# Eight tiles for unsearched attention weights, four for keys and values, in a planned transformer kernel

## The chip, the cores and the metric

The kernel runs on one core of one Trainium2 chip. Its metric is the device time of one execution in microseconds. Three runs of the kernel before gave 1355.88, 1356.01 and 1357.18 us; the median is 1356.01 us.

The core has four computing engines that run side by side, each through its own list of instructions, in order: TensorE (PE in the profile, with PEld for its weight loads), VectorE (DVE), ScalarE (ACT) and GpSimd (POOL). SyncE (SP) issues the DMA transfers. An engine waits on a semaphore when its next instruction needs something that another engine or a transfer has not finished.

## What is computed

Sixteen sequences (batches) of 256 tokens with 256 channels, 16 heads of 16 channels, all in float32. Every batch goes through two blocks. The first:

```python
m = silu(mod) @ w_ada + b_ada            # nine rows of shifts, scales, gates per batch
h = ln(x) * (1 + sc_msa) + sh_msa
x = x + self_attn(h) * g_msa             # rolled by 64, two windows of 128 tokens
h = ln(x) * (1 + sc_mca) + sh_mca
x = x + topk_cross_attn(h, context) * g_mca   # only the 16 largest scores of 256 per query
h = ln(x) * (1 + sc_mlp) + sh_mlp
x = x + swiglu(h) * g_mlp                # 256 -> 2 x 1024 -> 256
```

The second block is one more attention, over all 256 context tokens, without a search:

```python
xq, xkv = ada_ln(x_q, t, Wss_q), ada_ln(x_kv, t, Wss_kv)
x = x_q + softmax(q k^T / 4) v @ Wp      # q from xq, k and v from xkv
```

So a batch has three attentions: the windowed one ("self"), the searched one ("topk") and the last one ("last"). The two without a search exponentiate whole rows of scores; the searched one first finds the 16 largest scores of each row.

## The kernel before

**The planner.** The kernel does not issue its work as it is written down. Each piece of work, called an op, is recorded with its engine, a cost, the buffers it reads and writes, and a due time. `Plan.order` sorts the ops by due time (never before what they depend on), gives every buffer a tile from a fixed pool of its kind, and `Plan.run` issues them in that order. The due times are the table `DUE` at line 33: for each batch, stage and op one number in thousandths of a batch. One list serves all inner batches ("topk", "self", "prep", "last", "mlp"); batches 0, 1, 14 and 15 have lists of their own. Batch 15 is worked on in two halves of 128 tokens from its search on (`SPLIT`).

The order on every engine is therefore fixed when the program is built. A change of due times changes the order of instructions on all engines and the sequence in which tiles are handed out, but not the set of instructions.

Where the planner sees PE idle for more than 1 us ahead of an op, and a PSUM tile is free, it puts filler matmuls in (line 355, 128x512 on the identity), one per 0.87 us of the gap. They compute nothing that is used.

**The pools.** A kind of tile has a fixed number of copies (line 336 and the lines after it). An op that needs a tile waits until the last user of that copy has finished. Kinds that matter here:

- `pTO`: exponentials of the scores of an attention without search, 128 x 512. A round of four groups of heads (`exponentials`, line 631) fills four of them, and the product with the values (`weighted`, line 600) reads them.
- `k2`, `v`: keys and values. Each batch needs a pair for each of its three attentions.
- `pTT`: the same as `pTO` for the searched attention. `W`: the eight PSUM tiles, one bank each.

**The stages of a batch, by line.** Normalising: DVE statistics (444, 446), POOL (451 to 456), PE transpose (468), ACT (482). Products with weights: 494 (queries, keys), 530 (values), 577 (output projections). Self attention: scores for the row maxima (800), maxima on DVE (607), a small transpose (617), sixteen or eight tiny DMAs per batch that write the maxima into the queries (624), scores again (808), ACT exponentials (631), product with values (600), then DVE transpose and reciprocal (557, 559), POOL division (560), DVE transpose back (567). The last attention is the same with 952 for the first scores and 964 for the second. The searched attention: scores (847), four rounds a batch; each round has four groups, and each group runs MAX8 and MATCH_REPLACE on DVE twice (866, 874, 886, 891), ACT exponentials (879), a POOL product (895), PE transposes (544), an ACT copy (547) and the product with values (600). Feed-forward: 908 (up), ACT 918 to 927, POOL 925 and 928, and 935 (down). Line 935 is the last PE work of a batch's feed-forward and appears once per batch, so it is a convenient mark of the batches in the trace. Additions to x are on POOL (403, 418, 435), gate rows are scaled into weights at 423.

**Shapes on PE.** PE works in three shapes: the full array (products, transposes), four strips of 32 rows at once (scores: 800, 808, 847, 952, 964) and blocks of 17 output columns (600). The planner charges a switch between them:

```python
SWITCH = {128: 0.18, 32: 0.2, 33: 0.12}
```

A run of neighbouring PE instructions of one shape is called a group below. Loads of weights, of inputs, of gate rows and the tiny DMAs of line 624 all go through SP's one queue, in the planned order.

**The start.** Batch 0 has to go through its self attention before its search can begin, and most parameters are still arriving. The order there interleaves the products that make shifts, scales and gates (706 to 784) with the self attentions of batches 0 and 1.

Of the kernel before, what the change touches and what calls it, by code (L numbers as in the profile page):

```python
# [16 lines left out]
P = 128  # L17
B, L, C = 16, 256, 256
# [16 lines left out]
        -9570, -11657, -12085, -9792, -11847, -9363, -8686, -11839, -9345, -8419, -8682, -11836, -9366, -9397, -11886,  # L35
        -9644, -5321, -1682, -2688, -2632, -1153, -5643, -5425, -2469, -2565, -2724, -9446, -1295, -5757, -2172,
        -5835, -675, -1139, -1157, -5588, -2468, -1870, -5581, -1529, -1076, -1532, -1487, -5566, -1154, -5679, -1223,
        -5943, -106, 1074, 1255, 1393, -472, 224, 278, -1105, -1056, -1026, -5942, -321, -5710, 1347, 1352, -140,
        1081, -1522, -5590, -109, 361, 323, -32, -168, 342, -31, 913, 1389, 1308, 1596, 1753, -1138, -5554, -281,
        -5895,  # L40
    ),
    "self0": (
        -845, -8015, -9552, -8319, -8151, -7887, -2534, -12052, -7991, -11742, -12050, -12022, -11948, -11840, -11934,
        -3275, -11907, -3055, -9473, -9474, -9480, -9412, -3266, -5525, -5526, -5397, -5794, -5754, -1042, -734,
        -1323, -12229, -12179, -12027, -12419, -811, -9968, -9962, -7750, -10294, -872, -12484, -12372, -12192,
        -12320, -406, -10294, -9974, -8000, -5892, -279, -10035, -8044,
    ),
    "prep0": (
        -1155, -12001, -636, -12191, -12321, 410, -9381, 350, -10296, -8016, -7945, -7776, 17, -8420, 111, 261, -8435,
    ),  # L50
    "topk0": (
        397, 331, 117, 330, -8436, 336, 120, 355, -10058, 85, 137, 50, -9816, 51, 172, 25, -8473, -533, 366, 299, 554,
        -10042, 500, 388, 278, 408, -10013, 433, 352, 296, 656, -9074, -534, 523, 553, 595, -9922, 702, 689, 761,
        1066, 1337, 361, 191, 92, 596, -9842, 172, 593, 572, -10045, 536, 589, 451, 704, 130, 530, 577, -9912, 553,
        598, 477, 1093, -8997, 391, 619, 485, 774, -9093, 632, 758, 476, 825, -9242, 556, 633, 552, 1151, -9063, 1102,
        1333, 1338, 1363, 1359, 630, 657, 933, 787, -9141, 720, 1016, 886, -9062, 615, 311, 886, 687, 1092, 1065,
        1219, -9072, 827, 1092, 939, 1209, -8960, 1214, 1213, 1241, 1256, 1240, 1042, 1041, 956, 1089, -9068, 1260,
        1219, 558, 1258, 1240, 1243, 1336, 1337, 1323, 1360, 904, 1124, 1206, 1192, -9069, 1267, 734, 1266, 1211,
        1268, 732, 1329, 1167, 1208, 1029, 1273, 1241, 1261, 1270, 535, 1256, 1204, 1273, 1225, 1055, 1076, 1158,
        1334, 1060, 501, 1340, 1341, 1212, 1256, 502, 1330, 1342, 1353, 1342, 1338, 1367, 1253, 115, 1367, 1131, 1375,  # L60
    ),
    "self1": (
        -3755, -2639, -1238, -1452, -6312, -9036, -9099, -8976, -3443, -13366, -1419, -2386, -13023, -13295, -2081,
        -13301, -13346, -1223, -11030, -1380, -6922, -11295, -7021, -7022, -1205, -644, -687, -11297, -657, -640,
        -993, -1086, -420, -11042, -10382, -11043, -10445, -362, -337, -283, -523, -241, -592, -10816, -10820, -10821,
        -10843, -479, -383, -375, -641, -229, -299, -10068, -319,
    ),
    "prep1": (
        -1302, -13228, -265, -10135, -10120, -1180, -9435, 98, 263, -443, 200, 236, 209, 239, -265, 259, 335,
    ),  # L70
    "topk": (
        123, -321, 178, -60, 228, -226, -683, 166, 151, 153, -678, 173, 225, 164, -635, 88, -58, 396, 531, 633, 712,
        554, 222, 292, 305, 462, 289, -59, 382, 222, 445, 282, 432, 200, 547, 563, 21, 734, 631, 647, 342, 857, 536,
        530, 555, 569, 322, 566, 13, 510, 382, 573, 613, 588, 311, 524, 590, 603, 402, 591, 655, 585, 783, 202, 546,
        581, 633, 714, 610, 699, 712, 731, 779, 282, 659, 748, 349, 795, 525, 867, 596, 892, 941, 1119, 720, 807, 874,
        845, -622, 795, 460, 725, 394, 467, 593, 759, 489, 699, 505, 426, 488, 881, 1006, 804, 1080, 1060, 795, 963,
        913, 1113, 539, 794, 738, 345, 960, -663, 805, 736, 810, 965, -669, 1132, 726, 1018, 543, 1171, 914, 983, 912,
        1057, -908, 1011, 652, 1010, -909, 915, 834, 810, 1129, 1005, 453, 1074, -635, 1081, 1109, 376, 1158, 872,
        1032, 1006, 625, 1117, 920, 1017, 1051, 203, 1164, 872, 1060, 1051, 728, 1157, 710, 1190, 1181, 1210, 1226,
        1221, 240, 1264, 1232, 1243,  # L80
    ),
    "self": (
# [3 lines left out]
        -1907, -45,  # L86
    ),
    "prep": (
        9, 49, -1517, -1480, 156, -399, 268, 11, -190, -190, -375, 48, -1623, 245, 64, 65,
    ),  # L90
    "last": (
        1069, 1097, 1199, 1047, 1040, 1256, 1228, 1346, 1352, 1351, 1437, 1151, 2089, 1541, 1652, 1320, 2149, 1938,
# [1023 lines left out]
```

## Time and profile before

| | us |
|---|---|
| median of three runs | 1356.01 |
| the profiled execution, its time | 1355.89 |
| the profiled execution, span from first to last instruction | 1354.0 |
| PE busy | 1323.4 |
| DVE busy | 1213.5 |
| ACT busy | 1018.0 |
| POOL busy | 1026.5 |
| mean granted clock of TensorE, as a share of full speed | 0.993 |
| first line 935 (batch 0) starts | 164.11 |
| distance of two such marks, batches 0 to 12 | 79.27 (mean of twelve) |
| last line 935 (second half of batch 15) starts | 1317.82 |

The page gives for each engine its busy time, and the span in 40 slices; further views give busy times by stretch, single instructions in order of time, the waits of an engine with what ended them, and the chain of work that ended last. In the trace each matmul of the program appears as two records, so that 16 recorded L935 are 8 in the program (the half of a batch), and 32 a whole one. The idle time in square brackets behind a row is the engine's wait just before it, with the engine or transfer whose result ended it. Lines are those of the kernel before; the changed kernel's are two smaller.

### The profile page before, as it was taken

Reading aid. Unit: us, or ns where it says so; the run is one execution under the profiler, and the core shown is the slowest. Engines: PE = TensorE matmul, PEld = TensorE weight load, DVE = VectorE, ACT = ScalarE, POOL = GpSimd, SP = SyncE. Lnnn points to the kernel's source line nnn. Section 1 sums busy time; section 2 is a strip of 40 time slices with the busy share of each in tenths; the row PEclk is TensorE's granted clock in tenths of the full one; section 3 lists DMA queues with packets and bytes.
Section 4 is the critical chain, followed back from the end, with each engine's and each line's share of the span. In section 5 each row is a group of like instructions: output and inputs, shape, how many; then the busy total and the mean of one; then the engine's idle time right before and its main releaser. Section 6 shows DMA issues by size and latency. Waiting matters only on the chain.

```text
span 1354.0 us, 38576 instructions
## 1 busy us (share of the span) xinstructions
PE 1323.4 (98%) x13490; PEld 1029.2 (76%) x13490; DVE 1213.5 (90%) x4358; ACT 1018.0 (75%) x2359; POOL 1026.5 (76%) x1553
## 2 busy tenths in 40 slices
PE   8788999999999999999999999999999999999998
PEld 6566787878778787877878787787878778787885
DVE  5698999999999999999999999999999999999834
ACT  4466778787887878788787877878777787977783
POOL 1566887878788787878878787887878788778862
PEclk9898999999999999999999999999999999999999
DMA  5322001011100101110010111011011001000000
GB/s 166 105 67 95 21 17 26 25 26 33 26 25 18 24 27 26 33 25 21 22 24 27 26 33 26 12 29 24 29 26 34 23 20 33 19 2 2 17 2 18
DMA packets 64160, 42.44 MB, mean 31 GB/s; under 512 B 37763, under 2 KB 56751, under 8 KB 63711
## 3 DMA queue, kind: packets, MB, share of 16 engines
q1 hardware_dynamic: 63967, 39.99, 10.6%
q8 instruction: 107, 1.75, 0.5%
q14 instruction: 86, 0.70, 0.2%
HBM read 35.14 MB, written 4.29 MB: 29 GB/s over the span
## 4 chain that ended last, share of the span: by engine, by line
PE 87%; POOL 2%; DVE 2%; issue 1%; ACT 0%; POOLq 0%; DVEq 0%; ACTq 0%
PE W L908 17%; PE W L494 11%; PE W L600 11%; PE W L935 8%; PE W L544 8%; PE W L577 6%; PE W L530 5%; PE W L964 5%; PE W L952 5%; PE W L847 4%; PE W L468 3%; PE W L808 2%; PE W L800 2%; POOL prT L895 1%; PE W L355 0%
## 5 line engine op out<-in xcount | busy, mean ns | idle before, releaser
L895 POOL TENSOR_TENSOR prT<-rest,prT 128x512 f32<-128x512 f32 x256 | 325.4, 1275 | 31.5 <-DVE rest L891 23.1
L607 DVE TENSOR_REDUCE nm<-W 128x2 f32<-128x512 f32 (+1 forms) x384 | 237.6, 679 | 30.7 <-PE W L800 22.5
L879 ACT ACTIVATE prT<-W,ntop 128x256 f32<-128x256 f32 x512 | 214.0, 497 | 56.0 <-POOL ntop L868 49.1
L908 PE MATMUL W<-xT,w_L_xcond_w_m 128*128 128x256 f32 (+1 forms) x1088 | 251.2, 376 | 0.1
L631 ACT ACTIVATE pTO<-W 128x512 f32<-128x512 f32 (+1 forms) x392 | 199.8, 603 | 48.5 <-PE W L964 35.3
L908 PEld LDWEIGHTS W<-xT,w_L_xcond_w_m 128*128 128x128 f32 x1088 | 187.5, 190 | 61.5 <-ACT pTO L631 13.7
L874 DVE MATCH_REPLACE8 rest<-top,W 128x256 f32<-128x256 f32 x512 | 207.1, 412 | 0.0
L891 DVE MATCH_REPLACE8 rest<-top,rest 128x256 f32<-128x256 f32 x512 | 204.9, 408 | 0.0
L866 DVE MAX8 top<-W 128x8 f32<-128x256 f32 x512 | 184.3, 413 | 13.8 <-PE W L847 12.8
L886 DVE MAX8 top<-rest 128x8 f32<-128x256 f32 x512 | 185.3, 407 | 0.0
L547 ACT ACTIVATE pTT<-W 128x512 f32<-128x512 f32 x256 | 143.9, 628 | 8.3 <-PE W L544 8.3
L544 PE MATMUL W<-ident,prT 128*128 128x128 f32 x1024 | 137.3, 276 | 6.0 <-ACT prT L879 2.9
L925 POOL TENSOR_TENSOR mb<-ma,mb 128x256 f32<-128x256 f32 (+1 forms) x136 | 95.1, 699 | 53.7 <-ACT ma L920 37.3
L544 PEld LDWEIGHTS W<-ident,prT 128*128 128x128 f32 x1024 | 116.9, 141 | 24.0 <-POOL prT L895 3.8
L557 DVE STREAM_TRANSPOSE tr<-W 128x256 f32<-128x256 f32 (+1 forms) x162 | 78.2, 483 | 43.1 <-PE W L600 28.5
L560 POOL TENSOR_TENSOR on<-tr,rec 128x128 f32<-128x128 f32 (+1 forms) x162 | 71.7, 444 | 56.2 <-DVE rec L559 54.4
L935 PE MATMUL W<-w_L_xcond_w_m,h 128*128 128x256 f32 x512 | 113.6, 380 | 0.0
L935 PEld LDWEIGHTS W<-w_L_xcond_w_m,h 128*128 128x128 f32 x512 | 97.0, 190 | 13.8 <-POOL mb L925 0.7
L600 PE MATMUL W<-pTO,v 128*17 128x128 f32 (+1 forms) x2112 | 104.9, 323 | 0.1
L868 POOL TENSOR_SCALAR ntop<-top 128x2 f32<-128x2 f32 x256 | 52.7, 217 | 66.1 <-DVE top L866 61.6
L928 POOL TENSOR_TENSOR h<-h,mb 128x256 f32<-128x256 f32 (+1 forms) x136 | 94.8, 697 | 10.6
L418 POOL TENSOR_TENSOR x<-x,gated 128x512 f32<-128x512 f32 (+1 forms) x49 | 60.1, 1227 | 47.6 <-ACT gated L417 47.5
(129 smaller groups left out, 2665.6 us busy)
## 6 DMA issues: line engine op xcount, KB each, us to landing
gate<-gates SPq DMA_DIRECT2D x48, 256.0 KB
q<-nmT SPq DMA_DIRECT2D x480, 1.0 KB
cx<-in_ctx_dram SPq DMA_DIRECT2D x19, 256.0 KB
cx<-in_ctx_dram SPq DMA_DIRECT2D x104, 32.0 KB
rest<-in_L_xcond_w_ada_dram SPq DMA_DIRECT2D x9, 256.0 KB
x<-in_x_dram SPq DMA_DIRECT2D x16, 128.0 KB
x<-in_x_dram SPq DMA_DIRECT2D x32, 64.0 KB
w_L_xcond_w_m<-in_L_xcond_w_m_dram SPq DMA_DIRECT2D x1, 2048.0 KB
```

Source lines behind the costliest of these rows:

```text
L544: nc.tensor.transpose(w.t[:, ts(n, P)], flat[:, ts(n, P)], ident)
L600: nc.tensor.matmul(po.t[ds(NW * j, DH + 1), ds(q0, nq)], v.t[:, kt, 8 * m + 2 * j + a, :], pT.t.rearrange("p n q -> p (n q)")[:, ds(part, ...
L607: op("DVE", 0.61, lambda j=j, s=s: nc.vector.tensor_reduce(nm.t[:, k, ds(j, groups, step=4)], s.t.rearrange("p (g k) -> p g k", g=groups), ...
L631: op("ACT", 0.24 + q * 0.0005, lambda s=s, pT=pT: nc.scalar.activation(pT.t.rearrange("p n q -> p (n q)")[:, :q], s.t[:, :q], AF.Exp), r=[ ...
L866: nc.vector.max(top.t[:, a, 0:8], s.t[:, ts(a, L)])
L874: nc.vector.match_replace(rest.t[:, a, :], top.t[:, a, 0:8], s.t[:, ts(a, L)], TAKEN)
L879: nc.scalar.activation(pr.t[:, a, :], s.t[:, ts(a, L)], AF.Exp, bias=ntop.t[:, a:a + 1])
L886: nc.vector.max(top.t[:, a, 8:16], rest.t[:, a, :])
L891: nc.vector.match_replace(rest.t[:, a, :], top.t[:, a, 8:16], rest.t[:, a, :], TAKEN)
L895: op("POOL", 1.25, lambda: nc.gpsimd.tensor_tensor(pr.t, rest.t, pr.t, ALU.mult), r=[rest, pr], w=[pr])
L908: nc.tensor.matmul(w.t[:, :q], w_m1.t[:, c, ds(n0, P)], xT.t[:, c, :q], start=c == 0, stop=c == NCC - 1)
L935: nc.tensor.matmul(pp.t[:, ts(k, C)], hs[f].t[:, ts(k, P)], w_m2.t[:, f, :], start=f == 0, stop=f == NHC - 1)
```

## The change

Three pool sizes change, and the whole table of due times is replaced. There are eight tiles of `pTO` instead of five, four of `k2` instead of five, and four of `v` instead of five. In bytes per partition that is three times 2048 more and 4096 and 2176 less. The ops and their costs are the same.

```diff
 DUE = {
     "start": (
-        -9570, -11657, -12085, -9792, -11847, -9363, -8686, -11839, -9345, -8419, -8682, -11836, -9366, -9397, -11886,
+        -9079, -9474, -9247, -7795, -10959, -5686, -7231, -10933, -5595, -5764, -7671, -10944, -8055, -6777, -10987,
...
     "self": (
-        -1852, -383, -551, -1044, -1694, -2506, -2472, -1969, -746, -967, -952, -648, -716, -717, -644, -1050, -620,
+        -1974, -677, -761, -758, -1718, -1767, -1387, -1242, -787, -1974, -758, -688, -1415, -1974, -694, -590, -601,
...
     "mlp14": (
-        -14237, 1120, 1339, 1241, 1316, 1321, 1123, 1316, 1703, -413, -414, 1750, -224, 1638, -410, 1347, 1771, 1753,
+        -12321, 1209, 1239, 1104, 1103, 1325, 1411, 1103, 1534, 1182, 1202, 1524, 1204, 1580, 1410, 1613, 1680, 1475,
...
         "xT": (3, [P, NCC, L]), "q": (2, [P, NCC, L]), "q2": (2, [P, NCC, 2, L]),
-        "k2": (5, [P, NCC, 2, L]), "v": (5, [P, NT, NH, DH + 1]), "gate": (3, [P, 2, C]), "nm": (4, [P, NT, 32]), "nmT": (4, [P, NT, 32]),
+        "k2": (4, [P, NCC, 2, L]), "v": (4, [P, NT, NH, DH + 1]), "gate": (3, [P, 2, C]), "nm": (4, [P, NT, 32]), "nmT": (4, [P, NT, 32]),
         "top": (8, [P, 2, TOPK]), "ntop": (8, [P, 2]), "rest": (5, [P, 2, L]), "prT": (5, [P, 2, L]),
-        "pTT": (5, [P, 4, P]), "pTO": (5, [P, 4, P]), "tr": (3, [P, 16, NW]), "rec": (3, [P, 16]), "on": (3, [P, 16, DH]),
+        "pTT": (5, [P, 4, P]), "pTO": (8, [P, 4, P]), "tr": (3, [P, 16, NW]), "rec": (3, [P, 16]), "on": (3, [P, 16, DH]),
```

All lists of `DUE` are replaced in the same way. In the built program the order changes on all five engines. On PE the main differences are these, in the counts of the program:

- In the middle of the run, per batch: the two halves of the self attention's product with values (L600, 16 each) stand together and not apart, and some transposes (L544), value products (L530) and feed-forward blocks (L908) change places with neighbours.
- At the start: before the first search round, one L723 block, one L530 block and the L744 block of Wp move behind it; only one search round (L847) instead of two stands ahead of the second scores of batch 1 (L808); an L494 block of batch 2 moves ahead of the last transposes (L544) of batch 0's search. SP's queue is reordered with it.
- At the end: one L600 and one L964 block of batch 14 move from before the last L935 to behind it.

## The prediction

> **What bounds the kernel now.** I read the page first: engine shares and the forty slices.
>
> ```profile
> PE 1323.4 (98%) x13490; PEld 1029.2 (76%) x13490; DVE 1213.5 (90%) x4358; ACT 1018.0 (75%) x2359; POOL 1026.5 (76%) x1553
> PE   8788999999999999999999999999999999999998
> PEclk9898999999999999999999999999999999999999
> ```
>
> TensorE (PE) is full from the fourth slice to the last; VectorE (DVE) comes next. A share over the whole span hides stages, so the windows come second: one batch in the middle, then two stretches of the start and one just after them.
>
> ```profile
> 481.12:560.38 79.26, 79.26 (x822) 62.22 (x821) 74.96 (x270) 62.53 (x143) 64.81 (x98) 1.00 0.10 25
> 60.00:86.00 26.00, 20.70 (x215) 14.99 (x216) 23.75 (x95) 13.73 (x30) 12.27 (x15) 0.81 0.04 12
> 86.00:112.54 26.54, 18.69 (x164) 12.89 (x163) 26.54 (x114) 16.47 (x37) 22.70 (x37) 0.96 0.55 189
> 112.30:116.00 3.70, 3.70 (x11) 2.96 (x10) 3.70 (x17) 2.49 (x6) 0.37 (x2) 0.50 0.02 4
> ```
>
> After the span come PE, weight loads, DVE, ACT, POOL, the granted clock, DMA. In the middle PE is busy for all of 79.26 us, and the list of PE's waits for that window is empty; DVE has 4.3 us to spare. From 60 to 112 us it is the other way round: DVE is full (50.3 of 52.5) with the top-16 search of batch 0, and PE waits for it. The chain of waits closes it: 87% PE, and the feed-forward blocks at line 935 mark the batches, starting at 164.11 us (batch 0), then every 79.27 us to 1115.36 (batch 12), then 1189.97, 1261.39, 1296.40 and 1317.82 (batch 15, two halves). PE's useful matmuls are the same in both programs, so only four things can move the end: PE's idle time, its clock, the filler matmuls (line 355) and its switches between array shapes (128 rows; four of 32 rows; 17 columns).
>
> **The change part by part.** *Pools.* Five tiles of pTO become eight, five of k2 and v become four, and one memset of v goes. No instruction of a batch is added or removed; fillers go from 13 to 15. Everything else is order. I counted in the built order of the two programs.
>
> *The middle, twelve batches.* Shape groups go from 32 to 31 per batch. With eight pTO tiles both halves of the windowed attention can be in flight, so one lone L600 block (17 columns), which stood between a 128-row and a 32-row block, joins another. Price:
>
> ```profile
> 530.19 2.88 PE L908 MATMUL W<-xT,w_L_xcond_w_m 128*128 128x256 f32 x12
> 533.01 1.06 PE L600 MATMUL W<-pTO,v 128*17 128x256 f32 x16
> 552.84 1.07 PE L600 MATMUL W<-pTT,v 128*17 128x128 f32 x32
> 553.72 1.06 PE L600 MATMUL W<-pTO,v 128*17 128x128 f32 x32
> 554.71 1.14 PE L847 MATMUL W<-k,q 32*128 32x512 f32 x8
> ```
>
> First column start, second busy time. L600 before another L600 takes 553.72 - 552.84 = 0.88, before another shape 554.71 - 553.72 = 0.99: leaving costs 0.11. L908 x12 between two other shapes takes 533.01 - 530.19 = 2.82 against 12 x 0.216 = 2.59 (L577 x8 among its own kind: 1.73), again 0.11 per edge. The block after still enters its shape once, so one edge goes: 0.11 x 12 = **-1.3 us**. Ends: 0, and two edges, -2.6. Nothing fills PE's place here: the gain arrives only if no wait opens.
>
> *The start, to the first line 935 (164.11 us).* Matmuls and the 50 groups are equal; 10 fillers stand there instead of 5. DVE sets the pace, so what counts is when its search begins and when its last result lets PE go.
>
> ```profile
> 38.38 1.27 POOL L403 TENSOR_TENSOR x<-x,gate 128x512 f32<-128x512 f32 x1
> 39.60 0.62 POOL L560 TENSOR_TENSOR on<-tr,rec 128x256 f32<-128x256 f32 x1
> 54.03 0.75 DVE L866 MAX8 top<-W 128x8 f32<-128x256 f32 x2
> ```
>
> The chain to the first MAX8 runs through L560 on POOL, which before waits behind L403 (1.27); the new order swaps them. Two DVE pieces ahead of MAX8 move behind it (L729 directly in front, 0.34; L784, 0.41, earlier). From 0 to 1.27 + 0.34; I take **-1.4**, near the swap. DVE then does the same work up to the last group of batch 0, so the shift is carried.
>
> ```profile
> 107.14 1.43 PE L847 MATMUL W<-k,q 32*128 32x512 f32 x8
> 111.45 1.08 PE L544 MATMUL W<-ident,prT 128*128 128x128 f32 x4 [2.88 <-ACT prT L879]
> ```
>
> In that 2.88 us gap the new order puts an L494 block of the next batch (1.73): **-1.7**. Against it, one L723 block (0.97) and L744 of Wp (0.87), done in the idle stretch before, now come after it: **+1.8**. After the gap the window above shows a clock of 0.50 for 3.7 us, and 0.81 over the next 4: 3.7 x 0.5 + 4 x 0.19 = 2.6 us. A gap cut to about 1.1 us may avoid that; I take half, **-1.3**, ends 0 and -2.6. [...]
>
> On SP the sends of batch 1's maxima (L624, sixteen DMAs, 9.53 us of issue) now stand behind the 1 MB load of the second feed-forward weight, and w_kv goes behind 21 more issues. Of the sends: before, PE waited 7.04 us for them, and 8.4 us lay between their issue (53.94) and the first L808 (62.33). In the new order PE's blocks up to the second L800 of batch 1 sum to 45.7 us, and the maxima behind it end at 49.4: 4.5 us earlier. The sends then land at 57.8, the second search round follows at 62 to 64, and DVE, with four groups of 2.9 us from the first round, asks for it at 52.6 + 11.6 = 64.2: hidden, but by little. Of w_kv: 4.9 MB stand before it, 23 us at the 213 GB/s of the first 20 us; its first use is at about 25 us. 0 to +2, taken as 0, since DMA moved 368 GB/s at 100 to 108 us. Start: -1.4 - 1.7 + 1.8 - 1.3 = **-2.6**; ends +3.8 (only the +1.8 and the +2) and -4.1.
>
> *The end.*
>
> ```profile
> 1315.53 1.22 PE W L600 x16
> 1316.75 1.08 PE W L964 x16
> 1317.82 3.65 PE W L935 x16
> 1335.25 1.91 PE W L355 x4
> ```
>
> This is the chain. Behind the last L935 lie 29 us set by latency (norm, queries, maxima, sends, exponentials), in which PE runs 7.4 us of fillers. One L600 and one L964 of batch 14 move from before the last L935 to behind it: 0.99 + 1.07 = **-2.1**, hidden by that slack (fillers there fall from 8 to 4). From batch 13 to the last L935 the groups go from 91 to 82, one edge each: **-1.0**. One new filler stands between the halves of batch 15 where PE found other work before: **+0.9**. Together -2.2; ends 0 (the 29 us grow by what moves in) and -4.1 (no filler's time lost, two edges a group).
>
> Sum: -1.3 - 2.6 - 2.2 = -6.1 on the profiled execution of 1355.89 us (span 1354.0 and 1.9 around it), which is 0.12 under the median: about 1350.
>
> **The rivals.** (1) *VectorE sets the pace: slower.* The last search round of a batch (L847) starts 5.50 us ahead of L935 before (554.71 to 560.21); in the new order the blocks between sum to 4.63 (L847 1.07, L908 x4 0.96, L544 x16 0.87, L577 x8 1.73, in the trace's counts). It comes 0.87 us later, and its last results are already just in time:
>
> ```profile
> 496.81 1.27 POOL L895 TENSOR_TENSOR prT<-rest,prT 128x512 f32<-128x512 f32 x1
> 497.45 1.47 PE L544 MATMUL W<-ident,prT 128*128 128x128 f32 x12
> ```
>
> L895 ends at 498.08; the third group of that L544 is due at 498.32. If DVE's 4.3 us of slack lie elsewhere, the period follows the round: +0.87 x 12 = 10.4 instead of -1.3, so 1355.9 + 10.4 - 4.8 = 1361.5. It decides from 0.51 us per batch on (6.1 / 12). For it: that margin of 0.24, and the MAX8 of a batch wait 0.8 us for L847. Against: DVE was busy with older rounds for most of that stretch, and the new order holds no filler in the middle, as it would where a PE gap over 1 us was planned for. 0.21.
> (2) *Small waits eat the gain.* The second L600 of the merged pair starts 3.45 us after its scores begin; scores and exponentials take 3.25 (549.81 to 553.06). One copy of 0.5 us in front on ACT opens 0.3 us: 0.3 to 0.7 per batch gives 1353.5 to 1358. 0.09.
> (3) *The start gains nothing.* The 1 MB load (2.8 us at 368 GB/s) holds the sends, DVE runs dry before its second round, and the clock falls again: start 0 to +2.8, so 1352.6 to 1355.4. For it: the load is issued just ahead; against: some 3 us lie between. 0.14. [...]
>
> (4) *The clock falls with or without that gap.* Then only the -1.3 goes, and it is 1351.3. For it: clocks of 0.81 also stand in windows in which PE idled in small pieces; against: 0.50 right behind the gap. [...] 0.08.
>
> **How the numbers follow.** Forecast 0.48, with (4) 0.56. A change within 0.2% (2.7 us) can't be told from none. Faster: these and half of (3), 0.63. Same: (2) and the other half, 0.16. Slower: 0.21. The range: the low end has all gains at their ends (-2.6 - 4.1 - 4.1 = -10.8, 1345); the high end, 1361, reaches to rival (1). The forecast's own range, with (4), is 1345 to 1353.
>
> **What would show it.** Right: L935 of batch 0 near 161.5 us; twelve periods of 79.15; PE without waits between; the clock at 1.00 after about 110 us; the last L935 some 6 us before 1317.8; the 29 us behind it unchanged. Wrong: a wait before L544 or L600 in every period, with DVE or ACT as releaser, or a first L935 after 164 us.

## The result, and the profile after

The changed kernel takes 1350.85 us (median of six runs, 1350.28 to 1352.84), the kernel before, measured beside it, 1356.60 us (six runs, 1355.88 to 1357.89). The ratio is 0.9959, with a 95% interval of 0.9946 to 0.9972: 5.8 us faster. The profiled execution took 1350.46 us, its span 1348.6 us, 5.4 us less than the 1354.0 of before. The forecast of 1350.0 us holds for the total. Its three terms do not, and most of what follows is about that.

The page of the changed kernel, with the engine shares and two of the forty-slice rows:

```profile
PE 1323.5 (98%) x13494; PEld 1033.3 (77%) x13494; DVE 1217.5 (90%) x4358; ACT 1014.2 (75%) x2359; POOL 1020.9 (76%) x1552
PE   8889999999999999999999999999999999999998
PEclk9889999999999999999999999999999999999999
```

TensorE is as busy as before (1323.5 against 1323.4 us), in a span that is 5.4 us shorter: the page doesn't show what was gained. Marks do. The table takes the start of the L935 blocks (L933 in the changed kernel) from the rows in order of time, which put a mark 0.1 to 0.2 us earlier than the chain of waits that the prediction used.

| stretch | before | after | difference | forecast |
|---|---|---|---|---|
| start to the mark of batch 0 | 163.94 | 163.85 | -0.1 | -2.6 |
| batch 0 to batch 12 | 951.26 | 947.78 | -3.5 | -1.3 |
| batch 12 to the last mark | 202.55 | 200.55 | -2.0 | -2.2 |
| last mark to the end of the span | 36.2 | 36.4 | +0.2 | 0 |
| sum | 1354.0 | 1348.6 | -5.4 | -6.1 |

The start gave nothing, the middle gave more than twice what was forecast, and the end about what was forecast. Busy times in the changed kernel, in one middle period and in the two stretches of the start that were shown of before (span, PE, weight loads, DVE, ACT, POOL, granted clock, DMA):

```profile
479.92:558.88 78.96, 78.96 (x821) 62.41 (x820) 75.97 (x273) 62.42 (x143) 64.41 (x98) 1.00 0.10 26
60.00:86.00 26.00, 24.84 (x225) 15.49 (x224) 23.40 (x92) 13.18 (x29) 17.72 (x24) 0.79 0.36 127
86.00:112.00 26.00, 22.17 (x175) 16.39 (x174) 25.22 (x108) 16.32 (x37) 19.84 (x29) 0.93 0.22 59
```

A middle period is full for PE, as before, and 78.96 to 78.97 us long instead of 79.25. From 60 to 112 us the granted clock is 0.79 and 0.93, where it was 0.81 and 0.96. PE is some 7.5 us busier there: fillers take 5.1 us of these two stretches instead of 2.0, and the rest is other blocks, some of which stood before 60 us in the kernel before (without fillers PE is busy there for 43.3 us now, 46.8 before). The waits of PE between 40 and 125 us (us in total, times, longest) name what the start waited for:

```profile
PE W L353 <- ACT prT L877: 3.5, 1, 3.5
...
PE W L762 <- DMA rest<-in_L_xcond_w_ada_dram: 1.4, 1, 1.4
```

and the rows in order of time show what these waits did to the chain towards the first MAX8:

```profile
38.99 1.27 POOL L421 TENSOR_TENSOR gw<-w_L_xcond_w_so,gate 128x512 f32<-128x512 f32 x1 [4.11 <-DMA gate<-gates]
40.22 0.62 POOL L558 TENSOR_TENSOR on<-tr,rec 128x256 f32<-128x256 f32 x1
46.13 1.02 PE L762 MATMUL W<-rest,condT 128*16 128x256 f32 x4 [1.44 <-DMA rest<-in_L_xcond_w_ada_dram]
55.43 0.76 DVE L864 MAX8 top<-W 128x8 f32<-128x256 f32 x2 [2.43 <-PE W L845]
68.53 0.76 DVE L864 MAX8 top<-W 128x8 f32<-128x256 f32 x2 [1.41 <-PE W L845]
```

The swap on POOL that the prediction counted on did happen: L558 no longer stands behind the addition of L401. But the gate row that POOL needs first arrives at 38.99 instead of 37.13 us, so L558 starts later than before (40.22, not 39.60), and a 256 KB piece of w_ada, issued last in a row of loads, stops PE for 1.44 us at L762. The first MAX8 comes at 55.43 us: 1.40 later than before instead of 1.4 earlier. Not all of that is the order: the first scores of batch 0 (L798, L800 before), which stand ahead of all this, start at 16.72 us in this execution and at 15.90 in the one before. Counted from there the first MAX8 is 0.58 us later. The last row is the first MAX8 of the second search round: VectorE stands idle for 1.41 us before it.

The end of the chain of waits (start, length, block):

```profile
1308.26 1.85 PE W L598 x32
1310.24 1.15 PE W L962 x16
...
1312.25 3.67 PE W L933 x16
```

The last L933 starts 5.6 us earlier than L935 did at 1317.82; in front of it two L598 blocks now stand together and one L962 remains.

### The profile page after: what moved, and what is told of

It is laid out like the page before. It is cut to its first block, busy times and chain, and to the rows that moved or that the text cites. A ratio compares the mean times of both kernels' runs of the same rounds, so it can differ in the third digit from the quotient of the medians.

```text
span 1348.6 us, 38673 instructions
## 1 busy us (share of the span) xinstructions
PE 1323.5 (98%) x13494; PEld 1033.3 (77%) x13494; DVE 1217.5 (90%) x4358; ACT 1014.2 (75%) x2359; POOL 1020.9 (76%) x1552
## 4 chain that ended last, share of the span: by engine, by line
PE 92%; DVE 3%; SPq 1%; issue 1%; DMA 1%; ACT 1%; POOL 0%; POOLq 0%; DVEq 0%; ACTq 0%
PE W L906 17%; PE W L492 12%; PE W L598 11%; PE W L542 8%; PE W L933 8%; PE W L528 6%; PE W L575 6%; PE W L950 5%; PE W L845 5%; PE W L962 5%; PE W L466 3%; PE W L806 2%; PE W L798 2%; SPq L622 1%; DVE rest L872 1%
## 5 line engine op out<-in xcount | busy, mean ns | idle before, releaser
L605 DVE TENSOR_REDUCE nm<-W 128x2 f32<-128x512 f32 (+1 forms) x384 | 239.9, 682 | 30.9 <-PE W L798 17.4
L906 PE MATMUL W<-xT,w_L_xcond_w_m 128*128 128x256 f32 (+1 forms) x1088 | 249.1, 373 | 0.0
L629 ACT ACTIVATE pTO<-W 128x512 f32<-128x512 f32 (+1 forms) x392 | 198.8, 596 | 41.9 <-PE W L962 28.9
L906 PEld LDWEIGHTS W<-xT,w_L_xcond_w_m 128*128 128x128 f32 x1088 | 187.6, 190 | 52.3 <-ACT pTO L629 10.6
L864 DVE MAX8 top<-W 128x8 f32<-128x256 f32 x512 | 190.1, 420 | 15.7 <-PE W L845 12.8
L884 DVE MAX8 top<-rest 128x8 f32<-128x256 f32 x512 | 190.7, 418 | 0.0
L545 ACT ACTIVATE pTT<-W 128x512 f32<-128x512 f32 x256 | 148.7, 622 | 17.2 <-PE W L542 15.2
L542 PE MATMUL W<-ident,prT 128*128 128x128 f32 x1024 | 145.2, 277 | 4.4 <-ACT k L514 1.7
L542 PEld LDWEIGHTS W<-ident,prT 128*128 128x128 f32 x1024 | 117.9, 142 | 27.9 <-issue 6.2
L558 POOL TENSOR_TENSOR on<-tr,rec 128x128 f32<-128x128 f32 (+1 forms) x162 | 71.0, 443 | 67.8 <-DVE rec L557 67.5
L933 PE MATMUL W<-w_L_xcond_w_m,h 128*128 128x256 f32 x512 | 113.7, 379 | 0.0
L933 PEld LDWEIGHTS W<-w_L_xcond_w_m,h 128*128 128x128 f32 x512 | 97.0, 190 | 13.7 <-POOL x L416 0.3
L555 DVE STREAM_TRANSPOSE tr<-W 128x256 f32<-128x256 f32 (+1 forms) x162 | 78.4, 485 | 29.6 <-PE W L598 15.6
L598 PE MATMUL W<-pTO,v 128*17 128x128 f32 (+1 forms) x2112 | 102.2, 323 | 0.0
L921 ACT ACTIVATE mb<-W,half 128x256 f32<-128x256 f32 (+1 forms) x136 | 64.4, 489 | 31.7 <-PE W L906 31.6
```

The costliest lines, as they stand in the source:

```text
L542: nc.tensor.transpose(w.t[:, ts(n, P)], flat[:, ts(n, P)], ident)
L598: nc.tensor.matmul(po.t[ds(NW * j, DH + 1), ds(q0, nq)], v.t[:, kt, 8 * m + 2 * j + a, :], pT.t.rearrange("p n q -> p (n q)")[:, ds(part, ...
L605: op("DVE", 0.61, lambda j=j, s=s: nc.vector.tensor_reduce(nm.t[:, k, ds(j, groups, step=4)], s.t.rearrange("p (g k) -> p g k", g=groups), ...
L629: op("ACT", 0.24 + q * 0.0005, lambda s=s, pT=pT: nc.scalar.activation(pT.t.rearrange("p n q -> p (n q)")[:, :q], s.t[:, :q], AF.Exp), r=[ ...
L864: nc.vector.max(top.t[:, a, 0:8], s.t[:, ts(a, L)])
L884: nc.vector.max(top.t[:, a, 8:16], rest.t[:, a, :])
```

## The experiments

Theory, after the traces were compared: the middle gains by fewer and cheaper shape changes on PE; the start loses to late loads what its order gains; the end gains what moves behind the last L933. Rivals: the tiles themselves, not the order, give the gain; the start is set by PE's own work and not by the chain into the search; the tail pays for what moves into it. Marks are given as in the table above. Execution to execution the start differs by up to 3 us (below), so the middle and the end are read from single periods and stages, which repeat to 0.02 us.

**The pools alone.** The old due times also fit the new pools:

```diff
-        "k2": (5, [P, NCC, 2, L]), "v": (5, [P, NT, NH, DH + 1]), ...
+        "k2": (4, [P, NCC, 2, L]), "v": (4, [P, NT, NH, DH + 1]), ...
-        "pTT": (5, [P, 4, P]), "pTO": (5, [P, 4, P]), ...
+        "pTT": (5, [P, 4, P]), "pTO": (8, [P, 4, P]), ...
```

> The kernel before with the new pool sizes only (8 tiles of pTO, 4 of k2, 4 of v) and the old due times. Theory (the gain is the order): the order of the work stays, so 1.000 of the time before, within 0.2%; first line 935 at 164.1 us, period 79.27 us. Rival (the tiles themselves help, because exponentials find a free tile sooner): below 0.998, with a shorter period.

Measured: 1356.49 us (ten runs), ratio 1.0004 (0.9995 to 1.0013), period 79.24 us. The tiles alone give nothing; the gain is in the order. The merged pair of the middle does need them: its exponentials fill four tiles from 545.85 us and four more from 550.13 us (ACT L629), and the first product that reads any of them (L598) starts at 551.49 us. Whether the rest of the new order would run on five tiles was not tried.

**A lone 17-column block put back in the middle.**

```diff
-        -969, -968, -425, -138, -335, -332, ...
+        -969, -968, -425, -151, -335, -332, ...
```

> The changed kernel, in which one 17-column block of each batch goes back to stand alone between a 128-row and a 32-row block: 32 shape groups in a period again. Theory (one edge of 0.11 us, as the prediction priced it): period 78.97 becomes 79.08 us, 1.3 us over twelve. Rival A (all of the 0.30 us that a period gained comes from this merge): 79.27. Rival B (the merge is worth nothing, the gain is elsewhere): 78.97 to 78.99.

Measured: period 79.84 us, 0.87 us longer, worse than every theory. The rows of that run's period, PE and then ACT:

```profile
555.04 1.17 PE L806 MATMUL W<-q,k 32*128 32x128 f32 x32
556.15 0.66 PE L542 MATMUL W<-ident,prT 128*128 128x128 f32 x4
556.88 1.13 PE L906 MATMUL W<-xT,w_L_xcond_w_m 128*128 128x256 f32 x4
557.95 1.34 PE L598 MATMUL W<-pTO,v 128*17 128x128 f32 x31
...
560.20 1.14 PE L845 MATMUL W<-k,q 32*128 32x512 f32 x8
```

```profile
556.24 2.06 ACT L629 ACTIVATE pTO<-W 128x512 f32<-128x512 f32 x4 [1.22 <-PE W L806]
```

The two 17-column blocks take 2.25 us (557.95 to 560.20) instead of 1.87, because they start 2.91 us after their scores (L806 at 555.04) and the exponentials of those scores end only at 558.30. In front of them L906 starts 0.73 us after L542, and not 0.49. So of the 0.87 us, 0.38 and 0.24 are waits, and 0.11 is what the extra edge reads; most of the rest is that L906 block, 1.07 us long instead of 0.96. In the changed kernel the same margin is:

```profile
550.13 2.06 ACT L629 ACTIVATE pTO<-W 128x512 f32<-128x512 f32 x4 [0.23 <-PE W L806]
```

The exponentials end at 552.19, and the second half of the merged pair starts at 551.49 + 0.88 = 552.37: 0.18 us to spare. This is the prediction's rival of the small waits, which needed 3.25 us and had 3.45: it was close, and it did not happen.

**The same lone block, with the distance kept.** The four matmuls of one more L906 block go in front of the other 17-column blocks; middle fillers are switched off so that none is added.

```diff
-        -969, -968, -425, -138, -335, -332, ...
+        -969, -968, -425, -151, -335, -332, ...
-        1735, 1238, 1735, 1861, 1881, 1096, 1599, 1507, 1509, 1880, 1847, 1806, 859, 1648, 1897, ...
+        1735, 1238, 1735, 1861, 1881, 1096, 1599, 1507, 1509, 1880, 1847, 1806, 859, 1648, 1866, ...
-            if o.eng == "PE" and t - free["PE"] > IDLE and free["PE"]:
+            if o.eng == "PE" and t - free["PE"] > IDLE and free["PE"] and not 165 < t < 1200:
```

> The changed kernel with the lone 17-column block of the run before put back at the same place, and with one feed-forward block (line 906, four matmuls) moved ahead of the other 17-column blocks, so that these start about 3.9 us after their scores begin, as in the kernel before, instead of 2.9. Theory (of the 0.87 us that the period lost in that run, only the edge, 0.1, belongs to the number of groups; the rest was a wait for exponentials): period 79.0 to 79.1 us, against 78.97 and 79.84. Rival (a lone block itself is dear): 79.5 or more.

Measured: 80.01 us. A miss again. The waits for exponentials are gone (the pair takes 1.87 us), but others opened: L466 twice, behind the normalising on POOL (0.65 instead of 0.44 us, and 0.85 instead of 0.49), which itself starts 0.5 us later in the period after waiting 0.80 us for DVE L444, and L906 behind L542 (0.74 instead of 0.49). These make 0.21 + 0.36 + 0.25 = 0.82 of the 1.04 us; the edge again reads 0.11, and L906 is again 0.1 longer. The list of PE's waits is empty for this period; such short waits show only in the distances between the starts of the rows. Neither run isolates an edge as a whole-kernel time: the 0.11 is read from rows. What they show is that moving one 1-us block cost some seven to eight times its edge in waits elsewhere, and that the new table of due times merged the pair without opening such waits.

**What a 128-row group begins with.** Three groups of the period begin with a feed-forward block instead of transposes.

```diff
-        1556, 1289, ..., 1614, 1238, 1421, 1717, 1041,
-        1735, 1238, 1735, 1861, 1881, 1096, 1599, 1507, 1509, 1880, 1847, 1806, ...
+        1556, 1289, ..., 1614, 1238, 1421, 1711, 1041,
+        1735, 1238, 1735, 1856, 1881, 1096, 1599, 1507, 1509, 1880, 1847, 1801, ...
```

> The changed kernel, in which three 128-row groups of a period begin with a feed-forward block (line 906) instead of the transposes of line 542 that began them; the number of groups stays 31. In the traces a 128-row group between two edges takes 0.15 us more than its matmuls when transposes begin it, and 0.20 us when another block does. Theory (what begins the group sets the price of the edge): 78.97 becomes 79.12 us, 1.8 us over twelve. Rival (inside a group the order costs nothing): 78.97.

Measured: 79.13 us in every period from the second on, +0.16: the theory. One of the groups, first in the changed kernel, then in this run:

```profile
545.76 0.66 PE L542 MATMUL W<-ident,prT 128*128 128x128 f32 x4
546.25 1.03 PE L906 MATMUL W<-xT,w_L_xcond_w_m 128*128 128x256 f32 x4
547.12 1.89 PE L575 MATMUL W<-w_L_xcond_Wp,oT 128*128 128x256 f32 x8
548.94 1.17 PE L806 MATMUL W<-q,k 32*128 32x128 f32 x32
```

```profile
547.41 1.13 PE L906 MATMUL W<-xT,w_L_xcond_w_m 128*128 128x256 f32 x4
548.38 0.60 PE L542 MATMUL W<-ident,prT 128*128 128x128 f32 x4
548.81 1.89 PE L575 MATMUL W<-w_L_xcond_Wp,oT 128*128 128x256 f32 x8
550.64 1.17 PE L806 MATMUL W<-q,k 32*128 32x128 f32 x32
```

The same three blocks, from the start of the first to the start of L806: 548.94 - 545.76 = 3.18 us with the transposes first, 550.64 - 547.41 = 3.23 with them second. L542 takes 0.49 us first and 0.43 second, L906 0.97 first and 0.87 second: entering the shape costs 0.05 us with the transposes and 0.10 with L906. Why is not shown. One more group of the period changed, from L544 to L600 1.55 us in the kernel before and 1.46 in the changed one (L542 to L598), and no run tests it:

```profile
519.57 1.09 PE L544 MATMUL W<-ident,prT 128*128 128x128 f32 x8
520.56 0.63 PE L468 MATMUL W<-ident,xn 128*128 128x128 f32 x4
521.12 1.06 PE L600 MATMUL W<-pTO,v 128*17 128x256 f32 x16
```

```profile
518.52 1.09 PE L542 MATMUL W<-ident,prT 128*128 128x128 f32 x8
519.45 0.60 PE L466 MATMUL W<-ident,xn 128*128 128x128 f32 x4
519.98 1.06 PE L598 MATMUL W<-pTO,v 128*17 128x256 f32 x16
```

**The late piece, loaded sooner.** One load goes ahead of the loads of 34 to 41 us.

```diff
-        -644, 26, -8994, -144, 52, 10, -8772, ...
+        -644, 26, -8994, -144, -143, 52, -8772, ...
```

> The changed kernel, with one 256 KB load (the piece of w_ada for which line 762 waits 1.44 us at 46 us) issued ahead of the loads of 34 to 41 us instead of behind them; nothing else moves. Theory (the late piece costs the start): the wait goes, the first MAX8 comes at 54.0 to 54.4 instead of 55.43 us, VectorE carries that to the first line 933, at 162.7 to 163.0 instead of 164.01 us, and the ratio is 0.0008 to 0.0010 lower than that of the changed kernel (0.9959). Rival (VectorE's shift is not carried; TensorE's own work behind 119 us sets the mark): first MAX8 earlier, first line 933 still at 163.8 to 164.1.

Measured: 1346.80 us (1346.23 to 1348.06), ratio 0.9929 (0.9912 to 0.9946), some 4 us less than the changed kernel, three to four times what was expected. SP issues the piece at 37.80 us instead of 41.06, L762 doesn't wait, and the rows in order of time (start, length, what is done, and the wait before it in brackets) show the first MAX8 and the mark of batch 0:

```profile
54.79 0.76 DVE L864 MAX8 top<-W 128x8 f32<-128x256 f32 x2 [2.34 <-PE W L845]
```

```profile
160.51 4.70 PE L933 MATMUL W<-w_L_xcond_w_m,h 128*128 128x256 f32 x21
```

The first MAX8 is only 0.64 us earlier than in the profiled execution of the changed kernel, the mark of batch 0 is 3.34 us earlier. The traces of all runs show why. T is the start of the last L555 (L557 with the old lines) of batch 0's search, where its result leaves VectorE; the last column is the time at the granted clock 0.50 in the start.

| run | first scores | first MAX8 | T | mark of batch 0 | at 0.50 |
|---|---|---|---|---|---|
| before | 15.90 | 54.03 | 119.72 | 163.94 | 17.07 |
| pools alone | 16.52 | 54.72 | 120.30 | 164.53 | 17.07 |
| block in the gap (below) | 16.14 | 54.70 | 120.26 | 164.49 | 17.07 |
| changed kernel | 16.72 | 55.43 | 120.55 | 163.85 | 17.07 |
| turns not first | 17.03 | 57.82 | 121.45 | 164.78 | 13.65 |
| no filler in batch 15 (below) | 19.77 | 58.91 | 122.95 | 166.23 | 13.65 |
| scores back in front (below) | 16.93 | 55.62 | 120.36 | 163.65 | 13.65 |
| lone block back | 17.33 | 58.68 | 122.33 | 165.45 | 17.07 |
| lone block, distance kept | 17.82 | 56.19 | 119.66 | 163.21 | 10.24 |
| start without fillers (below) | 16.80 | 58.14 | 121.53 | 164.80 | 13.65 |
| one piece sooner | 17.25 | 54.79 | 117.22 | 160.51 | 3.41 |
| both pieces sooner | 15.55 | 52.69 | 117.44 | 160.72 | 13.65 |
| both pieces sooner, no fillers | 16.68 | 53.43 | 117.37 | 160.65 | 10.24 |
| both pieces sooner, more turns first | 15.84 | 52.20 | 115.73 | 159.80 | 10.24 |

First, the executions do not begin alike: the first scores, ahead of every load that these edits move, start between 15.55 and 19.77 us. So stretches are compared, not times. From the first scores to the first MAX8 it is 37.54 us with one piece sooner. Where the piece is late it is 37.3 us plus the wait at L762 in four runs (waits of 1.07, 1.36, 1.44 and 1.87 us), and 1.6 and 1.8 us more than that in the two runs in which the wait is 1.94 and 2.26 us and the clock is at 0.50 for 3.41 us behind it. So the chain gained 1.17 us, as expected, and 0.53 us of it went to a later beginning of this execution.

Second, from T to the mark it is 43.3 us in every run whose order is that of the changed kernel up to the mark (43.1 to 44.1 where the lists of the inner batches differ) and 44.2 in every one with the old order: from T on the shift of the search is carried one for one. From MAX8 to T it is not: that stretch varies from 62.4 to 65.7 us. VectorE is busy for 61.1 to 61.3 us of it in all the new starts and sets the pace; its idle time is 1.3 us with one piece sooner and 3.8 us in the changed kernel. Among the runs where nothing holds up L762 the stretch grows with the time at half clock: 62.43 us at 3.41, 63.53 and 63.94 at 10.24, 64.75 at 13.65, about 0.2 us per us. The four executions with one piece sooner agree: three have a mean clock of 0.999 and took 1346.23 to 1346.87 us, one has 0.996 and took 1348.06; 0.003 of the span is some 8 us at half clock. It is a relation between executions; nothing was run that changes the clock alone.

**Both pieces sooner.** The piece that stood between the sends and the store of the gate row goes ahead of the sends too.

```diff
-        -528, -1472, -8696, -179, -78, ...
-        -644, 26, -8994, -144, 52, 10, ...
+        -528, -1472, -8696, -317, -78, ...
+        -644, 26, -8994, -144, -318, 52, ...
```

> The changed kernel with two 256 KB loads of w_ada issued ahead of batch 0's sixteen sends (23 to 33 us on SP): the piece for line 762 and the one that stood between the sends and the store of the first gate row. Theory (the gate row on POOL, 38.99 us in the changed kernel and 37.13 before, is the next limit of the first MAX8): gate row at 37.5 to 38.5 us, first MAX8 at 53.2 to 54.3 (54.8 with one piece sooner), first line 933 at 159.0 to 160.5 us, ratio 0.992. Rival (the two loads push the sends and what follows back by as much as they gain): first MAX8 at 54.8 or later, ratio 0.993 or more.

Measured: the gate row at 37.44 us, the first MAX8 at 52.69 (the prediction's 52.6), the mark at 160.72 us; 1346.68 us, ratio 0.9925 (0.9910 to 0.9940). Of the 2.1 us by which the first MAX8 is earlier than with one piece sooner, 1.7 are an earlier beginning of this execution (15.55 against 17.25). The chain itself is 0.4 us shorter, and from MAX8 to T, with 10.2 us more at half clock, 2.3 us are lost. The gate row is not shown to be the limit: in the run with the same loads and no fillers (below) it comes at 38.86 us, and the first MAX8 still comes 36.75 us after the first scores, against 37.14 here. By time the two can't be told apart; both beat the changed kernel by 0.3%.

**The block in the gap, alone.** The prediction's L494 block goes into the 2.88 us gap of the kernel before, and nothing else changes.

```diff
-        1334, 1060, 501, 1340, 1341, ...
+        1334, 1060, 501, 1347, 1341, ...
```

> The kernel before, with one part of the change alone: a block of line 494 (1.73 us) goes into the gap of 2.88 us before the L544 at 111.45 us. Theory, as the prediction had it: 1.7 us for the block and 1.3 us (0 to 2.6) for the clock, so the first line 935 comes at 161.1 us (159.8 to 162.4) instead of 164.11, and the clock of 0.50 right behind 110.7 us is gone or shorter. Rival A (the clock falls all the same): 162.4 with 0.50 still there. Rival B (what waits behind that L544 sets the end, the block only changes places with a wait): 163.5 to 164.5.

Measured: 1356.48 us, ratio 1.0002 (0.9992 to 1.0011), mark at 164.49 us. The rows:

```profile
113.28 3.18 PE L494 MATMUL W<-xT,w_L_xcond_Wkv 128*128 128x256 f32 x8 [2.78 <-ACT prT L879]
116.26 1.06 PE L544 MATMUL W<-ident,prT 128*128 128x128 f32 x4
```

The wait did not shrink, it moved to the block. L494 reads xT and weights and nothing of the search, so what ACT L879 releases to it can only be its output tile: ACT L879 reads the search's scores out of a PSUM tile, and L494 needs one to write to. The wait before L544 ended in a wait for a bank as well: its data come from POOL, whose last L895 before it ended at 110.25 us, 1.2 us before L544 started. The clock falls behind the gap all the same: it is at 0.50 for 3.41 us from 113.93 us, as in the run with the pools alone and no block there (3.41 us from 113.52), against 6.83 us before.

**The fillers of the start.**

```diff
-            if o.eng == "PE" and t - free["PE"] > IDLE and free["PE"]:
+            if o.eng == "PE" and t - free["PE"] > IDLE and t > 165:
```

> The changed kernel without the filler matmuls of the start (ten in the program become none before 165 us; those of the end stay). Theory (the four that run from 58.96 to 62.67 us at half the clock stand in front of the second L806 block and hold up the second search round): that round starts about 1.3 us sooner, the first line 933 comes at 162.7 to 163.6 us. Rival (they keep the clock up): more time at the granted clock 0.50 than the 17.1 us of both kernels, first line 933 at 165 us or later.

Measured: 1350.03 us, ratio 0.9953 (0.9938 to 0.9968) against 0.9959; first MAX8 at 58.14, mark at 164.80 us, 13.65 us at 0.50. It can't be told from the changed kernel. The piece was late again in this execution (L762 waited 2.8 us), so the same edit was repeated on the kernel with both pieces sooner:

```diff
-        -528, -1472, -8696, -179, -78, ...
+        -528, -1472, -8696, -317, -78, ...
-        -644, 26, -8994, -144, 52, 10, ...
+        -644, 26, -8994, -144, -318, 52, ...
-            if o.eng == "PE" and t - free["PE"] > IDLE and free["PE"]:
+            if o.eng == "PE" and t - free["PE"] > IDLE and t > 165:
```

> The kernel with both pieces loaded sooner, without the filler matmuls of the start. Theory (the four fillers in front of the second L806 block only stand in the way, since they start after 3.4 us of waiting for a bank, when the clock has already fallen): the second search round starts 0.5 to 1.3 us sooner after the first MAX8, the first line 933 comes at 159.5 to 160.2 us, ratio 0.9918 to 0.9925. Rival (without them the clock stays down longer): half clock for longer than with them, ratio 0.993 or more.

Measured: 1346.76 us, ratio 0.9934 (0.9918 to 0.9951), mark at 160.65 us, second search round 12.6 us after the first MAX8 (12.1 with fillers). Neither theory shows in the time: the runs without fillers have no more time at half clock than those with them (13.65 against 17.07 us, 10.24 against 13.65), and are not faster. From the first scores to the mark the profiled executions give 143.97 us without and 145.17 with them where both pieces are sooner, and 148.00 and 147.13 where the piece is late: one execution each, so a us either way stays open. In the changed kernel a group of fillers itself waits 3.5 us, for a bank (the first line of its waits above; fillers read only the identity), and then runs at half clock.

**The filler between the halves of batch 15.**

```diff
-            if o.eng == "PE" and t - free["PE"] > IDLE and free["PE"]:
+            if o.eng == "PE" and t - free["PE"] > IDLE and free["PE"] and o.tag[0] != "mlp15":
```

> The changed kernel without the one filler (line 353, two matmuls of 512 columns, 0.86 us) between the halves of batch 15. Theory (the prediction's +0.9): the last line 933 comes at 1311.4 instead of 1312.25 us and the ratio is 0.0006 lower. Rival (the block behind it waits for data in any case): 1312.0 to 1312.3, ratio as before.

Measured: the stage between the two last marks is 18.61 us with and without it; ratio 0.9964 (0.9951 to 0.9977). Without the filler:

```profile
1299.74 0.38 PE L466 MATMUL W<-ident,xn 128*128 128x128 f32 x2
1300.78 2.18 PE L906 MATMUL W<-xT,w_L_xcond_w_m 128*128 128x128 f32 x16 [0.66 <-ACT xT L480]
```

From L466 to L906 it is 1.04 us without and 1.08 with the filler (1297.13 to 1298.21 in the changed kernel): it stands in a wait for xT and costs nothing. But that wait is new: before, L468 is followed after 0.31 us by scores (L952 at 1300.20 us), for which no such wait shows.

**Scores back in front of the last mark.**

```diff
-        3315, -1645, 3907, 2494, 2545, 1037, 1036, 4819, 3948, 3012, -1633, 3766, 5636, ...
+        3315, -1645, 3907, 2494, 2545, 1037, 1036, 4819, 3948, 3012, -1633, 3766, 5210, ...
```

> The changed kernel with one block of scores of batch 14 (line 962, 16 matmuls, 1.0 us) moved back from behind the last line 933 to in front of it, as in the kernel before. Theory (the tail behind the last line 933 is bound by latency and hides such blocks, so that each one moved behind it is worth its own length): the stage between the two last line 933 blocks takes 19.6 instead of 18.6 us, the tail stays at 36.2 to 36.5 us. Rival (the tail pays for what moves into it): the stage grows by 1.0 us and the tail shrinks by about as much, to 35.3.

Measured: the stage takes 20.97 us, +2.36, and the tail 36.4 us as in the changed kernel. The tail does hide the block: nothing of it comes back. In front of the mark it costs more than its length, since it takes 2.51 us there:

```profile
1311.76 2.58 PE L962 MATMUL W<-q,k 32*128 32x256 f32 x16
1314.27 3.72 PE L933 MATMUL W<-w_L_xcond_w_m,h 128*128 128x256 f32 x16
```

Its weight loads wait there for ACT L629, 0.8 us in four pieces.

**More groups that begin with transposes.** On both pieces sooner, five L542 blocks of a period come earlier, so that three more groups begin with transposes.

```diff
-        75, 3, 189, ..., 353, 414, 558, 675, -104, 128,
-        443, -349, ..., 630, 712, -106, 253, 325,
-        663, 746, 44, ...
-        1029, 960, 745, 776, 746, 903, 907, 736, 760, 415, 902, 909, ...
+        75, 3, 189, ..., 353, 414, 558, 598, -104, 128,
+        443, -349, ..., 630, 668, -106, 253, 325,
+        663, 711, 44, ...
+        1029, 960, 745, 776, 746, 896, 907, 736, 760, 415, 895, 909, ...
```

> The kernel of the run before, and in the middle three more 128-row groups of a period begin with transposes of line 542 whose input has long been written (by the trace of the changed kernel 1 us or more ahead). Theory (what begins a group sets the price of its edge, 0.05 us each): period 78.97 becomes 78.82 us, another 1.8 us over twelve, ratio 0.991. Rival (the transposes, brought forward, wait for a bank, or the block behind them for its scores): period 78.97 or more, ratio as in the run before or worse.

Measured: 79.85 us a period, 1359.89 us, ratio 1.0023 (1.0014 to 1.0033): the rival. Of the three edges one became 0.05 us cheaper, as expected (L542 and L906 x12 from one shape to the next, 3.18 us in place of 0.44 + 2.79); at the second the block of scores ahead of it (L962) takes 0.11 us longer, and at the third a wait stands, the largest part of the 0.87 us that a period lost:

```profile
557.63 1.99 PE L575 MATMUL W<-gw,oT 128*128 128x256 f32 x8 [0.56 <-ACT mb L921]
```

L575 reads nothing that ACT L921 writes; L921 reads a PSUM tile of L906. So it waits for a bank, as far as the releaser tells: with the transposes brought forward, none was free.

## Why the prediction was right, and where not

- **The middle, -1.3: right in kind, mis-sized.** It measured -3.5, outside the ends given (0 to -2.6). PE has no waits in a period, as forecast, and the period is 0.29 us shorter instead of 0.11. The term counted the groups and gave every edge one price. By the rows of one period the 0.29 us are 0.11 for the lone L600 block that joined another (the size that the term gave it, read from rows and not isolated by a run), some 0.10 because six and not four of the twelve 128-row groups begin with transposes, at the 0.05 us that the run on this measured, and 0.09 in one group of L544 and L468 (1.55 to 1.46 us), which no run tested. The period before batch 12's mark gained 0.2 us more (79.46 us before, now 78.96), and the first period 0.2 less.
- **The start, -2.6: wrong; -0.1 in the profiled execution.** Of its steps: the -1.4 for the first MAX8 failed. The swap on POOL was there, but two loads moved back on SP, and the chain from the first scores became 0.6 us longer (+1.40 from the beginnings of the two executions); the prediction checked w_kv and the sends, not the gate row and the pieces of w_ada. With both loads forward the chain is 1.0 to 1.8 us shorter than in the profiled execution before (36.4 to 37.1 us against 38.1), so the swap's size was about right. "The shift is carried" holds from T to the mark, and not from MAX8 to T, where 62.4 to 65.7 us were measured. The -1.7 for a block in the gap was wrong by itself: the gap ended in a wait for a PSUM bank, which a block in its place waits for as well (2.78 us for 2.88). In the changed kernel the place is better filled (two waits of 0.74 us), and from T to the mark it is 0.9 us shorter; how far the one makes the other was not taken apart. The clock's -1.3 did not come: the half clock behind 110 us is gone, as forecast, but as much stands earlier in the start, 17.07 us in both, and a us of half clock goes with 0.2 us, not 0.5, where VectorE sets the pace. The +1.8 for L723 and L744 is there (L742 at 125.64, L721 at 127.70 us).
- **The end, -2.2: -2.0 to the last mark and +0.2 behind it.** The -2.1 for the two blocks behind the last mark stands, and the tail hides them, as the run that moved one back shows. The filler's +0.9 was wrong for the filler, 0, but 0.7 of it is there as a wait for xT in its place (1.04 us against 0.31). The -1.0 for nine fewer groups is not to be found as a sum: the stage between the last two marks loses 2.8 us, but one more block of scores (L962, about 1 us) only moved from there one stage ahead, and the three stages before it grow by 0.30, 0.37 and 0.14 us. Two new waits of PE stand in the second of them (for sends at L806, 0.34, and for L605 at L542, 0.41) and two of before are gone from the third (0.22 and 0.49 at L468). What made the first one longer was not tried.
- **The rivals.** VectorE did not become the pace of the middle (75.97 of 78.96 us busy), though the last search round does start only 4.64 us ahead of the mark, as the prediction's sum said (the transposes in that sum are x8 in the trace's counts, not x16). The small waits did not open, with 0.18 us to spare. The third, that the start gains nothing, came true, and one part of its mechanism with it: VectorE ran dry before the second search round, which the prediction had called hidden, by 1.41 us in the changed kernel (0.85 to 2.03 in the runs with pieces sooner). The load, which that rival blamed, is not shown to be the cause. From the first send to the first L806 it is 8.29 us in the run with both pieces sooner and no fillers, where that load is issued 2.8 us ahead, 9.09 in the other run without fillers, and 8.39 before, with no such load: by these three executions it cost between nothing and 0.7 us.

The total was right by luck: the start's miss (+2.5) and the middle's (-2.2) nearly cancel.

## What to carry to other kernels

Ask of every wait that a moved block is to fill what it is for: when the releaser is an engine that only reads a PSUM tile, and the waiting block reads nothing that it wrote, the wait is for the bank, and a block put there that needs one inherits it, as L494 here (2.78 us, where L544 had waited 2.88). When a plan reorders a load queue, follow each load to its first user, also those that no engine waited for before (L762 here, 1.44 us). Where executions begin at different times (the first scores here at 15.55 to 19.77 us), compare stretches from a common block, not times. A price per edge taken from two blocks is a price of those two blocks (0.05 us into L542 here and 0.10 into L906, where the forecast had 0.11 for all): take it for each kind of neighbour before multiplying it by twelve.

## What was not expected of the hardware

The granted clock changes on a grid in these traces. In that of the kernel before, the stretches at 0.50 of the start last 10.24 and 6.83 us (from 59.44 and 110.64), in that of the changed kernel 6.83, 6.83 and 3.41 us (from 57.52, 74.59 and 101.89), and in all fourteen the time at 0.50 in the start is 1, 3, 4 or 5 times 3.413 us (last column of the table of runs). In the two traces the starts of such stretches lie whole multiples of 3.413 us apart: 51.20 us is 15 of them, 17.07 and 44.37 us are 5 and 13. These windows lie on the grid of the changed kernel's trace (columns as in the busy times above, the granted clock third from the right):

```profile
54.11:57.52 3.41, 1.18 (x9) 0.31 (x8) 2.09 (x8) 0.95 (x3) 2.07 (x3) 1.00 0.11 35
57.52:60.93 3.41, 1.97 (x3) 0.94 (x4) 3.41 (x16) 2.40 (x6) 1.11 (x6) 0.50 0.02 4
60.93:64.35 3.42, 3.42 (x35) 1.92 (x36) 3.42 (x16) 0.84 (x2) 1.27 (x1) 0.50 0.13 40
64.35:67.76 3.41, 3.41 (x52) 2.72 (x52) 2.77 (x12) 3.05 (x7) 1.27 (x1) 1.00 0.81 253
```

PE was busy for 1.18 of 3.41 us in the first, and the clock was 0.50 in the next two. Two later windows of the same trace show that the busy time of this view does not decide it alone:

```profile
71.17:74.58 3.41, 2.38 (x11) 1.30 (x10) 3.41 (x11) 2.70 (x7) 3.41 (x5) 1.00 0.06 24
91.65:95.07 3.42, 1.74 (x20) 1.27 (x22) 3.42 (x13) 2.48 (x6) 3.26 (x5) 1.00 0.00 0
```

The clock was 0.50 behind the first of them (74.59 to 81.41 us), with PE busy for 2.38 us, and 1.00 behind the second (to 101.88), with 1.74. What it goes by stays open. The four runs with the changed kernel's order up to the mark of batch 0 spend 13.65 to 17.07 us at half clock, a run in which one load moved spends 3.41, and with a first MAX8 earlier still (52.69 against 54.79 us) and 13.65 us at half clock the mark of batch 0 came no sooner (160.72 against 160.51).
